# Storing zeros in 22 steps, and holding the first weights of a layer's experts back: a change to a four-layer attention and mixture-of-experts kernel

## The chip, the cores and the metric

The kernel runs on one core of one Trainium2 chip. The core has five engines that run side by side, each with its own instruction stream in a fixed order: TensorE (PE, matmuls, with its weight loads shown as PEld), VectorE (DVE), ScalarE (ACT), GpSimd (POOL) and SyncE (SP). SP, ACT and POOL also issue DMA transfers; all of these run on the core's 16 DMA engines. An engine that has to wait on a semaphore holds everything behind it in its own stream.

The metric is the device time of one execution in microseconds (us), smaller is better.

## The reference: what is computed

The input `x` (2 sequences of 512 tokens, 256 features) passes four layers. Each adds a cross-attention with a context of 2 x 1024 tokens and then a mixture of 8 experts to the stream:

```python
x = x + L0_xattn(layernorm(x), ctx); x = x + L0_ffn(layernorm(x))   # 16 heads of 64, rotary keys; 1 of 8 experts
x = x + L1_xattn(ctx, layernorm(x)); x = x + L1_ffn(layernorm(x))   # 8 heads of 64; 1 of 8 experts and a shared one
x = x + L2_xattn(layernorm(x), ctx); x = x + L2_ffn(layernorm(x))   # 16 heads of 16, causal; 2 of 8 experts
x = x + L3_xattn(layernorm(x), ctx); x = x + L3_ffn(layernorm(x))   # 16 heads of 16, rotary; 2 of 8 experts
# an expert of layer 2, with gates from the two best logits of a token:
out = out + combine[..., e, None] * (relu(x @ w1[e].T) @ w2[e].T)
```

Everything is computed in float32.

## The kernel before

The 1024 tokens lie as 8 tiles of 128 rows in `X`. Each layer runs in two stages.

**Attention of layer 0.** 16 groups, each two heads of one sequence, run as one stream (`run_stream`, called at the end of the layer's block). A group has 4 steps; step `t` belongs to group `n = t // 4` and has place `u = t % 4` in it. In a step (`unit`) PE makes the scores of two key tiles (L862), ACT takes their exponential into `p` (L867), DVE clips `p` (L868) and adds it up (L873), and PE multiplies the `p` of the step before by the values (L793). Small pieces of other work are put between: the keys of the next group (`keys`: two projections, ACT copies them to `kT`, and SP exchanges the halves of each head into `turned` by four DMAs, L155), which `rotate` (L147 to L149) then combines on DVE and POOL at `u == 2`; and the end of the group before. For that end the sums of the exponentials go through `Inverse`: SP gathers them into a small tile (`inv<-sums`, L166), DVE takes the reciprocal (L169), SP writes it to DRAM (`inv<-inv`, L171) and reads it back spread over the partitions (`rec<-inv`, L174), and POOL multiplies (`divide`, L841). PE's own order is fixed as written (`pe_in_order`).

**Experts.** `slots_of` gives each token a row in a table of slots, 128 rows to a slot, and each slot belongs to one expert. `moe` scatters the normed tokens into the DRAM table `xd` by indirect DMAs from POOL, and then works slot by slot (`slot_tile`): the expert's weights come into a tile `w` (L438, from SP, for the first eight slots; an indirect DMA from POOL for the others), the rows come into `xs` (L447), two matmul stages follow, and the result goes to the table `yd` (layers 0 and 1: a plain store from ACT, L479). Afterwards `combine` gathers each token's row from `yd` (`yg`, L530, POOL) and adds it to `X`. Rows of the tables that no token fills must hold zeros (in layers 2 and 3 with a 257th column that says so). `fill_slots` writes these zeros: it is called in step 5 of layer 0's stream, makes a tile `zeros` of 128 x 257 on POOL, which waits for the queries of group 1 (`G[1]["ready"]`), and issues six DMAs from POOL (L655), of 1920, 128, 1920, 384, 2955.5 and 2955.5 KB.

**From layer 1's experts to layer 2's attention.** After the last slot of layer 1, `ahead16` projects layer 2's keys and values from the context: 8 key jobs (PE, then ACT into one of two tiles `sk`, L553, then a store from ACT to the DRAM tensor `kd`, L554) and 4 value jobs (DVE into `sv`, L601, store to `vd`, L603). Beside it `combine` gathers layer 1's results and DVE and ACT (`rsq`, L62) work out the next layernorm. Then `attend16` starts: it fetches `kT` (L1167) and `v` (L1171) of a group from `kd` and `vd`, transposes the normed rows (`pt`, L1252), projects queries (`pq`), and runs 8 groups. A group has a first pass that finds the maximum of each row (L1281 on PE, L1286 and L1287 on DVE), after which `with_maxima` adds the maxima to the queries (`qA`, L1302, DVE), and a second pass, one group later, with scores (L1338), exponentials (L1339), the causal mask on POOL (L1343) and the product with the values (L1314). At the end of a group the same `Inverse` runs with four small DMAs each way; its reciprocal on DVE and the division on POOL (L1353) are pinned in their engines' order.

**What sets the order of the work.** The kernel is written with a planner that keeps each engine's instructions in one fixed order, drawn up before the run from the program's order and estimated durations: an instruction whose inputs and buffers are free may be put ahead of others that stand earlier in the program. So the loads of layer 2's first four weight tiles (`slot_tile`, `s < 4`; the pool `L2g` has four buffers of them), which stand behind the whole attention of layer 2 in the program, are issued from SP ahead of it. `tc.add_manual_dep` adds an edge by hand: with `Sync` the later instruction waits on a semaphore for the earlier one, with `NoSync` only the order on the engine is fixed.

Of the kernel before, what the change touches and what calls it, by code (L numbers as in the profile page):

```python
# [33 lines left out]
def tile_kernel(ctx: ExitStack, tc: tile.TileContext, d: dict, out: bass.AP):  # L34
# [143 lines left out]
    def add_bias(bias):  # L178
        nc.vector.tensor_add(X, X, bias[:, None, :].to_broadcast([P, TT, D]))
# [223 lines left out]

    def moe(L, ps, hp, ep, rows, slots, wrow, used, F, act, glu, finish, filler=None):

# [29 lines left out]
        def slot_tile(s):  # L435
            w = ep.tile([P, WC], F32, tag="w", name="w")
            if s < E:
                nc.sync.dma_start(w, wd[s * P : (s + 1) * P, :])  # L438
            else:
                nc.gpsimd.indirect_dma_start(  # L440
                    out=w, out_offset=None, in_=wd,
                    in_offset=bass.IndirectOffsetOnAxis(ap=wrow[:, s - E : s - E + 1], axis=0),
                )
# [194 lines left out]

    def fill_slots(ins):

        zeros = const.tile([P, D + 1], F32, tag="zeros", name="zeros")
        z = nc.gpsimd.memset(zeros, 0.0).ins
        tc.add_manual_dep(
            z, ins.name, mybir.DependencyInfo(mybir.DependencyClass.Sync, mybir.DependencyReason.DATA),
            reason="transfers that nothing waits for yet",
        )
        nc.gpsimd.tensor_scalar(zeros[:, D:], c_part, 2.0 * NT, None, ALU.add)
        for L, NS, RW in (("L0", 15, D), ("L1", 15, D), ("L2", 23, D + 1), ("L3", 23, D + 1)):
            rows = NS * P + (2 * NT if RW > D else 0)
            xds[L] = [  # L650
                dram.tile([NS * P, RW], F32, tag=f"{L}xd", name="xd"), dram.tile([rows, D], F32, tag=f"{L}yd", name="yd")
            ]

            for to in xds[L][:1] if RW > D else (xds[L][0], xds[L][1][(E + ALWAYS[L]) * P :, :]):
                nc.gpsimd.dma_start(  # L655
                    to.rearrange("(s p) f -> p s f", p=P),
                    zeros[:, None, 0 : to.shape[1]].to_broadcast([P, to.shape[0] // P, to.shape[1]]),
                )

# [11 lines left out]
    with (  # L671
# [186 lines left out]
        def scores(n, kt):  # L858
# [7 lines left out]
            p = G[n][f"p{kt}"] = tmp.tile([P, 2, N], F32, tag="p", name="p", bufs=5)  # L866
            nc.scalar.activation(p, s1, AF.Exp, scale=0.125)  # L867
            nc.vector.tensor_scalar(p, p, EXP_HI, EXP_LO, ALU.min, ALU.max)  # L868
# [6 lines left out]
        def unit(t, pieces):  # L875
# [25 lines left out]
            if t == 5:  # L901
                fill_slots(G[1]["ready"])
                add_bias(bo)
            for _ in range(3):
                pieces()

        for _ in prep(0, first_keys()):
            pass
        nx, nctx = norm_of(X, 4, 4, True), norm_of(C, 8, 8)
        with pe_in_order():  # L910
# [274 lines left out]
    def attend16(L, params, nkt, causal, rotary, bias, first=None, late=None):  # L1185
# [11 lines left out]
        with (  # L1197
# [17 lines left out]
            G = [dict() for _ in groups]  # L1215
            oTs = {}

# [78 lines left out]
            def with_maxima(n):  # L1296

                pt = bank("nmT")
                for qt in range(4):
                    nc.tensor.transpose(pt[:, qt * P : (qt + 1) * P], nms[n % 2][:, qt, :], ident)  # L1300
                qA = kp.tile([P, N], F32, tag="qA", name="qA")
                nc.vector.tensor_add(qA, pt, G[n]["qT"])  # L1302
                G[n]["qA"] = qA
# [90 lines left out]
            with pe_in_order():  # L1394
                while t <= NG * slots + LAG + 6 or pieces.queue:
# [33 lines left out]
                    elif h % 2 or 2 * pieces.left > slots - h or n >= NG:  # L1429
                        pieces()  # L1430
                    t += 1

    ctxr = ExitStack()
# [36 lines left out]

    attend16("L2", params, 4, True, False, True)
    pre.close()
# [3 lines left out]
    with (  # L1476
# [17 lines left out]

        yd = moe("L2", ps, hp, ep, xn, slots, wrow, used, 1024, AF.Relu, False, plain, next_keys)
        add_results(results(ap, yd, 0, 4), gates, X, range(4))
# [244 lines left out]
```

## Time and profile before

| | |
|---|---|
| median of 3 runs | 2299.71 us (2297.59 to 2301.05) |
| the profiled execution's own time | 2299.66 us |
| its span in the profile | 2297.9 us |
| granted TensorE clock, mean | 0.957 of full |
| PE busy | 2098.3 us, 91% of the span |
| DMA moved | 301.22 MB, mean 131 GB/s |
| of it on SP's queue (q1) / POOL's (q0) / ACT's (q10) | 159.79 / 115.00 / 24.39 MB |

How to read what follows. In a line of the order of time, the columns are the start, the time from the first start to the last end, the engine, the line of the kernel, the operation, what it writes and reads, the number of instructions, and in brackets the idle time ahead of it with what ended it. `SPq` and `ACTq` mark instructions that issue a DMA. In a line of the stage table, the columns are the stretch, its length, the busy time of PE, PEld, DVE, ACT and POOL with their instructions in brackets, the clock that TensorE was granted (1.00 is full), the share of the 16 DMA engines that was busy, and GB/s. A shape such as 128x512 is partitions by elements.

### The profile page before, as it was taken

The page shows a single profiled execution, that of the slowest core. Times are in us where ns is not written, and L with a number is a line of the kernel's source. Part 1 is how long each engine was busy: PE and PEld are TensorE (multiplying, and loading weights), DVE is VectorE, ACT ScalarE, POOL GpSimd, SP SyncE. Part 2 cuts the span into 40 slices and gives each one's busy share as a digit, 9 for nine tenths or more (in the row PEclk, how much of TensorE's full clock was granted, in tenths as well). Part 3 has the DMA queues.
Part 4 walks back from the last instruction along what each step waited for, and adds up shares of the span by engine and source line. Part 5 has one row for each costly group of instructions (what it writes and reads, how often), then busy time and mean ns, then how long its engine had stood idle before and what let it go on. Part 6 is the DMA issues. An engine that isn't in the chain of part 4 may idle for free. (4 is left out here: it accounts for less than half of the span.)

```text
span 2297.9 us, 30714 instructions
## 1 busy us (share of the span) xinstructions
PE 2098.3 (91%) x11892; PEld 1270.5 (55%) x11892; DVE 1088.6 (47%) x2161; ACT 864.4 (38%) x1657; POOL 447.3 (19%) x426
## 2 busy tenths in 40 slices
PE   7899999989998999999897898999699999669996
PEld 3344444448984444554585434589533333569985
DVE  7466766651114665665312675211377773422223
ACT  4344444431114655555111233322125556223333
POOL 3133322210002111211101022312122220021210
PEclk9999999999999999999899899999889999789998
DMA  6511111267845101001455311688410101547872
GB/s 189 157 33 47 33 28 28 87 238 272 308 166 149 47 28 37 28 10 33 171 200 222 129 48 41 215 296 321 140 48 23 35 20 25 238 166 311 315 298 63
DMA packets 104392, 301.22 MB, mean 131 GB/s; under 512 B 23088, under 2 KB 66352, under 8 KB 95536
## 3 DMA queue, kind: packets, MB, share of 16 engines
q1 hardware_dynamic: 76624, 159.79, 20.7%
q0 software_dynamic: 12544, 115.00, 13.5%
q10 hardware_dynamic: 15072, 24.39, 2.8%
q8 instruction: 98, 1.61, 0.3%
q14 instruction: 54, 0.44, 0.1%
HBM read 243.42 MB, written 47.66 MB: 127 GB/s over the span
## 5 line engine op out<-in xcount | busy, mean ns | idle before, releaser
L1339 ACT ACTIVATE p<-s 128x512 f32<-128x512 f32 (+3 forms) x384 | 185.9, 545 | 179.3 <-PE s L1338 118.8
L132 PE MATMUL pa<-sT,w 128*128 128x128 f32 x1920 | 235.9, 277 | 10.2 <-DVE sT L457 4.1
L132 PEld LDWEIGHTS pa<-sT,w 128*128 128x128 f32 x1920 | 227.3, 193 | 18.6 <-ACT sq L1519 5.8
L475 PE MATMUL y<-w,hT 128*128 128x256 f32 x960 | 219.8, 381 | 7.7 <-DVE hT L472 4.9
L1281 PE MATMUL s<-kT,qT 32*128 32x512 f32 (+3 forms) x768 | 217.5, 604 | 9.3 <-DVE nm L1287 4.8
L1338 PE MATMUL s<-qA,kT 32*128 32x512 f32 (+3 forms) x768 | 196.2, 585 | 0.7 <-DVE qA L1302 0.4
L475 PEld LDWEIGHTS y<-w,hT 128*128 128x128 f32 x960 | 177.3, 190 | 32.1 <-DVE hT L472 6.8
L1291 DVE TENSOR_REDUCE mx<-s 128x1 f32<-128x512 f32 x256 | 163.3, 684 | 56.2 <-PE s L1281 35.6
L472 DVE TENSOR_TENSOR hT<-act,pg 128x512 f32<-128x512 f32 x82 | 56.2, 687 | 236.4 <-PE pg L132 208.2
L867 ACT ACTIVATE p<-s 128x1024 f32<-128x1024 f32 x128 | 124.1, 1021 | 101.8 <-PE s L862 101.7
L132 PE MATMUL pg<-sT,w 128*128 128x128 f32 x1312 | 160.2, 275 | 1.7 <-ACT sv L570 1.7
L1026 ACT ACTIVATE p<-s,nm 128x512 f32<-128x512 f32 x192 | 129.3, 685 | 83.5 <-DVE nm L1023 83.5
L132 PEld LDWEIGHTS pg<-sT,w 128*128 128x128 f32 x1312 | 153.4, 192 | 1.9 <-ACT sv L570 1.9
L1023 DVE TENSOR_REDUCE nm<-s 128x2 f32<-128x1024 f32 x96 | 113.2, 1220 | 82.0 <-PE s L1019 81.9
L868 DVE TENSOR_SCALAR p<-p 128x1024 f32<-128x1024 f32 x128 | 109.6, 864 | 86.8 <-ACT p L867 86.8
L149 POOL TENSOR_TENSOR kT<-kT,turned 128x512 f32<-128x512 f32 x62 | 99.8, 1615 | 213.9 <-DVE turned L147 207.1
L793 PE MATMUL o<-p,v 128*64 128x512 f32 x512 | 127.5, 614 | 14.6 <-DVE p L868 14.5
L873 DVE TENSOR_TENSOR acc<-acc,p 128x1024 f32<-128x1024 f32 x96 | 131.8, 1373 | 2.8
L862 PE MATMUL s<-qT,kT 64*128 64x512 f32 x512 | 128.1, 619 | 0.0
L1314 PE MATMUL o<-p,v 128*32 128x256 f32 (+3 forms) x1280 | 106.6, 404 | 6.8 <-POOL p L1343 6.6
L1040 PEld LDWEIGHTS pt<-ident,p 128*128 128x128 f32 x768 | 85.6, 141 | 49.0 <-issue 23.8
L1281 PEld LDWEIGHTS s<-kT,qT 32*128 32x128 f32 x768 | 75.8, 188 | 66.0 <-issue 27.3
(284 smaller groups left out, 2981.5 us busy)
## 6 DMA issues: line engine op xcount, KB each, us to landing
w<-in_L_experts_dram SPq DMA_DIRECT2D x8, 3200.0 KB
w<-in_L_experts_dram SPq DMA_DIRECT2D x8, 3072.0 KB
w<-in_L_experts_dram SPq DMA_DIRECT2D x8, 2048.0 KB
w<-in_L_experts_dram SPq DMA_DIRECT2D x8, 1536.0 KB
kd<-sk ACTq DMA_DIRECT2D x40, 256.0 KB
kT<-kd SPq DMA_DIRECT2D x16, 512.0 KB
turned<-kT SPq DMA_DIRECT2D x60, 128.0 KB
v<-vd SPq DMA_DIRECT2D x12, 512.0 KB
```

The costliest lines, as they stand in the source:

```text
L132: nc.tensor.matmul(ps_ap, lhsT[:, dc, lcols], rhs[:, dc, rcols], start=(dc == 0), stop=(dc == 1))
L475: nc.tensor.matmul(y, hT[:, f, :], w2[:, f, :], start=(f == 0), stop=(f == FT - 1))
L793: nc.tensor.matmul(G[n]["o"][64 * j : 64 * j + 64, :], V[g, b][:, kt, pr * P + 64 * j : pr * P + 64 * j + 64], p[:, j, :], start=(kt == 0) ...
L862: nc.tensor.matmul(s1[:, j, :], G[n]["kT"][r, kt * P : (kt + 1) * P], G[n]["qT"][r, :], start=True, stop=True)
L867: nc.scalar.activation(p, s1, AF.Exp, scale=0.125)
L873: nc.vector.tensor_add(G[n]["acc"], G[n]["acc"], p)
L1023: nc.vector.tensor_reduce(nm[:, qt, :, c], s1, AX.X, ALU.max, negate=True)
L1026: nc.scalar.activation(p[:, j, :], s1[:, j, :], AF.Exp, bias=nm[:, qt, j, c : c + 1], accum_out=l[:, qt, j, c : c + 1],)
L1281: nc.tensor.matmul(s1[:, :w], qT[r, qt * P : (qt + 1) * P], kT[r, c * 512 : c * 512 + w], start=True, stop=True)
L1291: nc.vector.tensor_reduce(mx[:, qt, j, c : c + 1], s1, AX.X, ALU.max)
L1338: nc.tensor.matmul(s2[:, qs], kT[r, kt * P : (kt + 1) * P], qA[r, qs], start=True, stop=True)
L1339: nc.scalar.activation(p[:, j, qs], s2[:, qs], AF.Exp, scale=0.25)
```

## The change

Two parts.

1. `fill_slots` becomes a generator. It is started before the stream: it makes `zeros` on POOL, without the wait for group 1's queries, creates the tables, and lists the regions to fill in pieces of at most 512 rows (22 pieces). Then, in every odd step after step 5, it is handed the last exponential of the step and stores one piece, by a DMA from ACT that stands behind this exponential in ACT's order. The pieces come to 10.5 MB as before.
2. `attend16` returns the first instruction that writes a `qA`. For layer 2, `moe` gets it as `hold`, and the loads of the first four weight tiles wait for it with a semaphore.

```diff
--- before.py
+++ after.py
@@ -401,7 +401,7 @@
 
     ALWAYS = {"L0": 6, "L1": 4, "L2": 11, "L3": 13}
 
-    def moe(L, ps, hp, ep, rows, slots, wrow, used, F, act, glu, finish, filler=None):
+    def moe(L, ps, hp, ep, rows, slots, wrow, used, F, act, glu, finish, filler=None, hold=None):
 
 
 
@@ -435,7 +435,12 @@
         def slot_tile(s):
             w = ep.tile([P, WC], F32, tag="w", name="w")
             if s < E:
-                nc.sync.dma_start(w, wd[s * P : (s + 1) * P, :])
+                x = nc.sync.dma_start(w, wd[s * P : (s + 1) * P, :]).ins
+                if hold is not None and s < 4:
+                    tc.add_manual_dep(
+                        x, hold.name, mybir.DependencyInfo(mybir.DependencyClass.Sync, mybir.DependencyReason.DATA),
+                        reason="not among the transfers that the attention waits for",
+                    )
             else:
                 nc.gpsimd.indirect_dma_start(
                     out=w, out_offset=None, in_=wd,
@@ -636,15 +641,13 @@
     dram = ctx.enter_context(tc.tile_pool(name="slots", bufs=1, space=bass.MemoryType.DRAM))
     xds = {}
 
-    def fill_slots(ins):
+    def fill_slots():
+
 
         zeros = const.tile([P, D + 1], F32, tag="zeros", name="zeros")
-        z = nc.gpsimd.memset(zeros, 0.0).ins
-        tc.add_manual_dep(
-            z, ins.name, mybir.DependencyInfo(mybir.DependencyClass.Sync, mybir.DependencyReason.DATA),
-            reason="transfers that nothing waits for yet",
-        )
+        nc.gpsimd.memset(zeros, 0.0)
         nc.gpsimd.tensor_scalar(zeros[:, D:], c_part, 2.0 * NT, None, ALU.add)
+        todo = []
         for L, NS, RW in (("L0", 15, D), ("L1", 15, D), ("L2", 23, D + 1), ("L3", 23, D + 1)):
             rows = NS * P + (2 * NT if RW > D else 0)
             xds[L] = [
@@ -652,10 +655,18 @@
             ]
 
             for to in xds[L][:1] if RW > D else (xds[L][0], xds[L][1][(E + ALWAYS[L]) * P :, :]):
-                nc.gpsimd.dma_start(
-                    to.rearrange("(s p) f -> p s f", p=P),
-                    zeros[:, None, 0 : to.shape[1]].to_broadcast([P, to.shape[0] // P, to.shape[1]]),
-                )
+                todo += [to[r : min(r + 4 * P, to.shape[0]), :] for r in range(0, to.shape[0], 4 * P)]
+        ins = yield
+        for to in todo:
+            x = nc.scalar.dma_start(
+                to.rearrange("(s p) f -> p s f", p=P),
+                zeros[:, None, 0 : to.shape[1]].to_broadcast([P, to.shape[0] // P, to.shape[1]]),
+            ).ins
+            tc.add_manual_dep(
+                x, ins.name, mybir.DependencyInfo(mybir.DependencyClass.NoSync, mybir.DependencyReason.DATA),
+                reason="transfers that nothing waits for yet",
+            )
+            ins = yield
 
     def psum(tags, name):
 
@@ -864,7 +875,7 @@
                 )
 
             p = G[n][f"p{kt}"] = tmp.tile([P, 2, N], F32, tag="p", name="p", bufs=5)
-            nc.scalar.activation(p, s1, AF.Exp, scale=0.125)
+            G[n]["exp"] = nc.scalar.activation(p, s1, AF.Exp, scale=0.125).ins
             nc.vector.tensor_scalar(p, p, EXP_HI, EXP_LO, ALU.min, ALU.max)
             if kt == 1:
                 G[n]["acc"] = tmp.tile([P, 2, N], F32, tag="acc", name="acc")
@@ -899,13 +910,19 @@
             if t == 0:
                 pieces.add(second_batch(nx, nctx), 9)
             if t == 5:
-                fill_slots(G[1]["ready"])
                 add_bias(bo)
+            if t > 5 and t % 2 and n < len(groups):
+                try:
+                    fills.send(G[n]["exp"])
+                except StopIteration:
+                    pass
             for _ in range(3):
                 pieces()
 
         for _ in prep(0, first_keys()):
             pass
+        fills = fill_slots()
+        next(fills)
         nx, nctx = norm_of(X, 4, 4, True), norm_of(C, 8, 8)
         with pe_in_order():
             run_stream(len(groups), 4, 3, unit, prep, lambda n: 3 + 2 * (groups[n][2] == 0))
@@ -1213,7 +1230,7 @@
 
             groups = [(b, g) for b in range(B) for g in range(4)]
             G = [dict() for _ in groups]
-            oTs = {}
+            oTs, ready = {}, []
 
             def fetch(n):
                 g = groups[n][1]
@@ -1299,7 +1316,7 @@
                 for qt in range(4):
                     nc.tensor.transpose(pt[:, qt * P : (qt + 1) * P], nms[n % 2][:, qt, :], ident)
                 qA = kp.tile([P, N], F32, tag="qA", name="qA")
-                nc.vector.tensor_add(qA, pt, G[n]["qT"])
+                ready.append(nc.vector.tensor_add(qA, pt, G[n]["qT"]).ins)
                 G[n]["qA"] = qA
 
             def product(n, kt, half=None):
@@ -1429,6 +1446,7 @@
                     elif h % 2 or 2 * pieces.left > slots - h or n >= NG:
                         pieces()
                     t += 1
+            return ready[0]
 
     ctxr = ExitStack()
     crp = ctxr.enter_context(tc.tile_pool(name="ctxr", bufs=1, reuse_waits="tile"))
@@ -1468,7 +1486,7 @@
         combine(hp, yd, slots, None, X)
 
 
-    attend16("L2", params, 4, True, False, True)
+    hold = attend16("L2", params, 4, True, False, True)
     pre.close()
     pre, params = params16("L3", True, False)
     ap = pre.enter_context(tc.tile_pool(name="L3a", bufs=1, reuse_waits="tile"))
@@ -1492,7 +1510,7 @@
             ahead16(ps, fp, "L3", params, 8)
             first.update(first_of16(ap, "L3", params, 8))
 
-        yd = moe("L2", ps, hp, ep, xn, slots, wrow, used, 1024, AF.Relu, False, plain, next_keys)
+        yd = moe("L2", ps, hp, ep, xn, slots, wrow, used, 1024, AF.Relu, False, plain, next_keys, hold)
         add_results(results(ap, yd, 0, 4), gates, X, range(4))
         late = results(ap, yd, 4, 4), gates
 
```

## The prediction

> **What bounds the kernel now.** I read the page first, for where TensorE (PE) is not busy; then the stage table of the first 150 us and of 1190 to 1330 us, because the change touches these two places; then, in both, the order of time of PE, SP, ACT and POOL; last the waits in the undisturbed part of layer 0, for the slack that the moved stores will meet.
>
> ```profile
> span 2297.9 us, 30714 instructions
> PE 2098.3 (91%) x11892; PEld 1270.5 (55%) x11892; DVE 1088.6 (47%) x2161; ACT 864.4 (38%) x1657; POOL 447.3 (19%) x426
> 80.00:90.00 10.00, 4.64 (x20) 2.04 (x19) 0.31 (x1) 3.11 (x4) 1.53 (x2) 0.89 0.62 156
> 90.00:100.00 10.00, 5.69 (x16) 1.53 (x16) 9.97 (x8) 1.73 (x2) 7.49 (x4) 0.60 0.00 0
> ...
> 350.00:400.00 50.00, 49.88 (x196) 21.47 (x192) 33.62 (x36) 21.57 (x28) 16.29 (x10) 1.00 0.13 32
> ...
> 1240.00:1250.00 10.00, 5.82 (x14) 2.28 (x12) 0.00 (x0) 0.00 (x0) 2.86 (x3) 0.92 1.01 426
> 1250.00:1260.00 10.00, 5.60 (x8) 1.86 (x8) 5.82 (x22) 2.86 (x4) 5.76 (x7) 0.74 0.59 217
> ```
>
> PE is the bound almost everywhere (49.88 of 50 us in the middle of layer 0's stream). So only a place where PE stands is worth anything: one at 84 us, one from 1245 to 1283 us, both beside a saturated DMA share (1.01 to 1.04). The first, by the order of time of SP and PE:
>
> ```profile
> 62.15 2.01 SPq L166 DMA_DIRECT2D inv<-sums  x2
> 74.43 0.35 SPq L171 DMA_DIRECT2D inv<-inv  x1
> 83.48 1.10 SPq L174 DMA_DIRECT2D rec<-inv  x2
> 84.67 2.46 SPq L155 DMA_DIRECT2D turned<-kT  x4
> ...
> 94.31 1.98 PE L793 MATMUL o<-p,v 128*64 128x512 f32 x4 [9.67 <-DVE p L868]
> ```
>
> The four big zero stores and two small ones, issued by POOL from 39.8 to 55.9 us, hold the DMA engines until 83 us. Meanwhile the inverse's round trip on SP takes 21 us (62.15 to 83.48), where later groups need 4 (212.35, 214.93, 216.38). SP issues in order, so the exchange `turned<-kT`, whose keys were copied by 69.7 us, leaves at 84.67. DVE stands 11.0 us before the rotation, the clipping of `p` is queued behind it, and PE waits 9.67 us for `p`. The second place, by SP, ACT and POOL:
>
> ```profile
> 1233.95 28.37 SPq L438 DMA_DIRECT2D w<-in_L_experts_dram  x4
> ...
> 1246.50 0.95 POOL L530 DMA_INDIRECT yg<-yd,si  x1 [35.32 <-DMA w<-in_L_experts_dram]
> ...
> 1251.09 0.69 ACT L553 ACTIVATE sk<-pk,bk 128x512 f32<-128x512 f32 x1 [11.41 <-DMA kd<-sk]
> 1259.73 0.21 ACT L62 ACTIVATE rsq<-rsq 128x4 f32<-128x4 f32 x1 [2.43 <-DVE rsq L61]
> 1260.51 0.69 ACT L553 ACTIVATE sk<-pk,bk 128x512 f32<-128x512 f32 x1 [0.57 <-ACT rsq L62]
> 1271.23 0.69 ACT L553 ACTIVATE sk<-pk,bk 128x512 f32<-128x512 f32 x1 [7.20 <-DMA kd<-sk]
> ...
> 1278.03 2.07 PE L1252 MATMUL pt<-ident,xn 128*128 128x128 f32 x8 [2.48 <-DVE xn L98]
> ```
>
> The four weight tiles of layer 2 (2048 KB each) leave at 1234, though nothing uses them before the xs of layer 2's experts arrive at about 1480 us. Under them the last `yd` store, issued at 1234.27, lets the gathers start only at 1246.50; in layer 0 the same step took 2.6 us (last `yd` store 681.9, first `yg` 684.5). The `kd` stores hold both `sk` buffers, ACT waits 11.41 and 7.20 us, PE's four PSUM banks fill and PE stops.
>
> **The change part by part.** The sum is made against the profiled execution, 2299.66 us (span 2297.9 and 1.8 around it); the median of the runs shown, 2299.71, is the same.
>
> *Zeros: the burst goes.* PE gets back the gaps 9.67, 0.56 (100.65) and 0.18 (101.91). It also gets back the half clock behind them: eight score matmuls in 2.87 instead of 1.99 us, four product matmuls in 1.98 instead of 1.08, together 1.78. That is 12.2 us. Without the burst the exchange leaves at about 70 us and the rotation has 15 us more than now. The gaps at 52.7 and 54.7 (1.22, 0.90) stay: there DVE is busy 9.90 of 10 us.
>
> *Zeros: 22 smaller stores come.* 10.5 MB in pieces of 512 rows (4+1, 4+1, 6, 6 of them), on every odd step from 7 to 49, one per 13 us, on ACT's queue behind the second exponential of the step. Nothing is queued on a semaphore there: `zeros` is ready long before. ACT's issue: no such store is in the trace; the nearest rows are 0.33 us (`kd`, 256 KB) and 0.52 (`C`, 512 KB from SP in 1 KB rows); 22 x 0.5 = 11 us of ACT. It is covered by ACT's own waits right after that exponential (2.69 us before `kT`, 1.27 before `ou`, at 219.02 and 236.23); without that cover it is at most 11. On the DMA engines a piece takes 512 KB / 284 GB/s (the rate at 60 to 70 us) = 1.9 us, 2.25 at the slowest slice of the burst (233). Who can be hit: in each group's second step the piece starts at about 216.4 (exponential 214.39 + 1.94), the `rec` loads run from 216.38 and the exchange leaves at 219.66. The reader of `rec`, POOL at 219.84, is needed by the matmuls `po` at 224.41, 3.3 us after it ends; behind the exchange POOL's product ends at 227.6 and its sum starts at 230.03, 2.4 us of slack (0.7 in the group at 245, whose sum then has 3.7 before its first scores). So 1.9 us fits. Bounds: 0 (more transfers cannot help) and 22 x 2.25 = 50. I take 1, near the covered end. POOL loses six DMA issues (6.9 us), on no path: its next product at 41.91 waited for its exchange, issued 37.35 to 39.85, anyway. The early memset stands on POOL before anything else is due there; its second step waits for `route`, issued at 16.2, and POOL's next work is at 41.9.
>
> A rule weighed here: the Trainium skill, "DMA: Bandwidth & Descriptors", section "Queues, rings and completion order", says that each DMA engine takes turns packet by packet between the queues that have work. By it a store on POOL's queue would hardly hold up two 2 KB reads on SP's queue, the stall at 84 us would have another cause and stay, and the sum would be about 11 us smaller. The trace differs: those reads, on another queue, kept DVE 11.4 us.
>
> *Hold: the stage before layer 2's attention.* Without the weights the gathers start 2.6 us after 1234.27, at 1236.9, 9.6 us earlier. In ACT's order the square root `rsq` stands between the fourth and the fifth `sk`, and it waits for these gathers: fifth `sk` at 1260.51 - 9.6 = 1250.9. With free stores one `sk` follows another every 1.72 us (layer 3's keys, 1452.32 to 1457.47), so the eighth is at 1256.1 instead of 1271.23. From there to the transposes `pt` it is 6.8 us now, of which 1.8 is half clock (eight value matmuls in 3.57 instead of 1.78). So `pt` comes at 1261.1 instead of 1278.03: 16.9 us. The first `pq` runs in 3.12 us now and 1.91 warm: 1.2 more. Together 18.1. Bounds: 14 if the stores still lose some 4 us, 21 if the planner puts `rsq` behind the keys (then eight keys from 1235.25 take 13.8 us, the values 7.1, and `pt` is at 1257 to 1258).
>
> *Hold: the weights inside the attention.* They now wait for the first `qA`, which ends at 1297.2 by the old clock. What stands behind them on SP: `kT` of group 3 (1313.00) and the inverse's trips (`inv<-ou` at 1317.51, then DVE's reciprocal and POOL's division, both pinned in their engines' order, with the maxima and the masks of PE's work behind them). The earlier fetches leave at 1279 to 1283, before `qA`. 8.39 MB at the 425 GB/s of 1238 to 1250 us are 19.7 us, with 2 for latency they end 21.7 after `qA`; `inv<-ou` comes 20.3 after. It is late by 1.4, and POOL already waits 1.62 us for `rec` at 1328.12, so there is no slack: I take 2. Bounds: 0, and 11 if the rate is the burst's 284 GB/s (31.5 after `qA`). Weights in by 1320 are not missed at 1480.
>
> Sum: -12.2 + 1 - 18.1 + 2 = -27.3; 2299.66 - 27.3 = 2272.4, forecast 2272.
>
> **The rivals.**
> 1. *The weights in front of the attention's own transfers.* Price 11 instead of 2: 2281; if the second weight pair also drags, with `kT` of group 3 late, 2284. For it: one queue, no slack in `rec`. Against: at 1240 to 1250 the same transfers ran at 426 GB/s.
> The Trainium skill, same page and section, says that an engine consumes one ring's descriptors in order; by that rule `inv<-ou` could not pass the weights at all. No row here shows two SP transfers passing or not passing.
> 2. *Each fill costs the stream its own length* (ends slower). Place: the exchange and `rec` of each group, and ACT's exponentials; price up to 2.25 us x 22 = 50: 2299.66 - 27.3 - 1 + 49.5 = 2321. It decides from 28.3 / 22 = 1.3 us each; 0.5 each would give 2282. For it: the burst showed that stores on one queue delay small transfers on another far beyond their size. Against: 2.4 to 3.7 us of slack, and a piece that is over when the exchange leaves.
> 3. *The stall at 84 us stays*: it is only DVE's backlog (9.90 of 10 us busy at 50 to 60). Then 2272 + 11 = 2283. Against: DVE is busy 2.71 of 10 at 60 to 70 and waits.
> 4. *The hold changes nothing*: the planner fills the gap with other transfers, or the stores are slow by themselves. Then 18 - 2 = 16 are missing: 2288. Against: `kd` stores at 1452 to 1471, at 231 to 261 GB/s of total traffic, flow every 1.72 us.
>
> **How the numbers follow.** The forecast's case 0.60 (its own range 2265 to 2279, from the bounds 14 and 21 of the hold and 0 and 3 of the fills and collisions); rival 1 0.12; rival 2 0.13, of which 0.07 with 0.5 us each and 0.06 slower; rival 3 0.06; rival 4 0.05; both gains gone or eaten 0.04. The range 2262 to 2286 takes in the forecast, rivals 1, 3 and the mild 2, and leaves out about 0.15. 0.2% (4.6 us) is about what a measurement of this kernel tells from no change: faster 0.88, same 0.04, slower 0.08 (strong rival 2, and a part of the last case).
>
> **What would show it.** Right: no PE gap over 2 us from 60 to 110; `inv<-sums` to `rec` in about 4 us; POOL's queue smaller by 10.5 MB, ACT's larger; `yg` within 3 us of the last `yd`; no wait of `sk` over 3 us; the four weights issued together some 20 us before `inv<-ou`. Wrong: waits of POOL on `turned` or `rec` that grow on odd steps; `inv`'s reciprocal or POOL's division standing more than 5 us in layer 2's first groups; `sk` still waiting for `kd`.

## The result, and the profile after

The changed kernel takes 2271.27 us (2269.58 to 2272.57) against 2298.65 us before: a ratio of 0.9884, with a 95% interval of 0.9864 to 0.9905. The forecast was 2272, in a range of 2262 to 2286. The profiled execution took 2271.06 us, its span is 2269.0, and the mean granted clock is 0.962 (before: 0.957).

From the page, the span, the busy time of the engines, and the queues of POOL (q0) and ACT (q10):

```profile
span 2269.0 us, 30730 instructions
PE 2087.4 (92%) x11892; PEld 1267.6 (56%) x11892; DVE 1085.2 (48%) x2161; ACT 866.2 (38%) x1657; POOL 438.6 (19%) x420
...
q0 software_dynamic: 9888, 104.49, 12.0%
q10 hardware_dynamic: 25664, 34.90, 4.3%
```

The 10.5 MB of zeros are on ACT's queue now (24.39 to 34.90 MB), and off POOL's (115.00 to 104.49). PE does the same 11892 matmuls in 10.9 us less busy time, at a mean granted clock of 0.962 instead of 0.957. From the stage table (columns as before), the two places that the change touches, and the stretch that holds the 22 stores:

```profile
80.00:90.00 10.00, 10.00 (x44) 3.56 (x43) 9.90 (x10) 5.45 (x7) 3.21 (x2) 1.00 0.24 79
90.00:100.00 10.00, 10.00 (x34) 3.66 (x34) 4.60 (x6) 3.94 (x7) 1.27 (x1) 1.00 0.43 126
...
1270.00:1280.00 10.00, 8.79 (x68) 3.60 (x65) 8.55 (x23) 4.17 (x12) 2.80 (x7) 1.00 1.01 429
...
85.00:385.00 300.00, 299.10 (x1152) 126.02 (x1150) 201.13 (x214) 131.39 (x165) 89.26 (x55) 1.00 0.25 70
```

From 80 to 100 us PE is busy all the time at full clock; before, it was busy 4.64 and 5.69 of 10 us there, at 0.89 and 0.60. Over the 300 us with the stores it misses 0.9 us. The saturated DMA share (1.01), which stood at 1240 to 1250 before, now stands at 1270 to 1280, inside layer 2's attention, and PE works under it.

In layer 0, the order of time of SP, the first inverse and the exchange behind it:

```profile
61.53 1.17 SPq L166 DMA_DIRECT2D inv<-sums  x2
...
66.32 1.10 SPq L174 DMA_DIRECT2D rec<-inv  x2
69.13 2.45 SPq L155 DMA_DIRECT2D turned<-kT  x4
```

From `inv<-sums` to `rec` it is 4.8 us instead of 21.3, and the exchange leaves at 69.13 instead of 84.67. From layer 1's last slot to layer 2's attention, by ACT, POOL and PE (the lines of `sk`, `yg` and `pt`; the first line is the last store of a `yd`):

```profile
1217.29 0.33 ACTq L484 DMA_DIRECT2D yd<-yo  x1
...
1219.77 0.95 POOL L535 DMA_INDIRECT yg<-yd,si  x1 [25.58 <-DMA yd<-yo]
...
1226.78 0.69 ACT L558 ACTIVATE sk<-pk,bk 128x512 f32<-128x512 f32 x1 [2.39 <-DMA kd<-sk]
...
1233.55 0.69 ACT L558 ACTIVATE sk<-pk,bk 128x512 f32<-128x512 f32 x1 [0.28 <-ACT rsq L62]
...
1238.05 0.69 ACT L558 ACTIVATE sk<-pk,bk 128x512 f32<-128x512 f32 x1 [0.94 <-PE pk L132]
...
1244.84 1.63 PE L1269 MATMUL pt<-ident,xn 128*128 128x128 f32 x8 [1.69 <-DVE xn L98]
```

The gathers start 2.48 us after the last store instead of 12.23, the longest wait of `sk` for `kd` is 2.39 instead of 11.41, and PE stands 1.69 us before `pt`.

How the weights held the key stores in the kernel before shows in the packets of the two queues, here from 1240 to 1250 us (queue, packets, MB, share of the 16 engines; q1 is SP's queue with the weights, q10 is ACT's with the key stores):

```profile
q1 hardware_dynamic: 267, 3.85, 90.2%
q10 hardware_dynamic: 270, 0.39, 10.4%
```

Both queues move the same number of packets, as if they took turns, but a packet of the weights is ten times as large. So the stores get a tenth of the engines' time, and the gathers and `sk` wait for them.

In the attention, by SP and POOL:

```profile
1265.36 2.30 SPq L438 DMA_DIRECT2D w<-in_L_experts_dram  x4
...
1285.55 2.46 SPq L166 DMA_DIRECT2D inv<-ou  x4
1290.87 0.34 SPq L171 DMA_DIRECT2D inv<-inv  x1
1292.45 1.72 SPq L174 DMA_DIRECT2D rec<-inv  x4
...
1295.90 1.27 POOL L1370 TENSOR_TENSOR oT<-ou,rec 128x512 f32<-128x512 f32 x1 [1.35 <-DMA rec<-inv]
```

The four weight tiles leave 20.2 us before `inv<-ou`. From `inv<-ou` to the division it is 10.35 us, before 10.61 (1317.51 to 1328.12), and the division's wait for `rec` went from 1.62 to 1.35: nothing is late.

Where the time went, by PE's order: when a mark is reached in each kernel, and what the difference gained since the mark above. A mark is the start of the matmuls named, an attention's end is the start of the routing's first matmul behind it, and the last mark is an end.

| mark on PE | before | after | difference | since the last mark |
|---|---|---|---|---|
| layer 0, first sums of exponentials | 60.47 | 59.84 | -0.6 | -0.6 |
| layer 0, second sums | 101.91 | 88.49 | -13.4 | -12.8 |
| layer 0, end of its attention | 501.10 | 487.10 | -14.0 | -0.6 |
| layer 1, last `y` of the experts | 1231.84 | 1214.85 | -17.0 | -3.0 |
| layer 2, first `pt` | 1278.03 | 1244.84 | -33.2 | -16.2 |
| layer 2, first transposed maxima | 1293.21 | 1261.29 | -31.9 | +1.3 |
| layer 2, end of its attention | 1448.31 | 1413.88 | -34.4 | -2.5 |
| layer 2, last `y` of the experts | 1635.09 | 1603.69 | -31.4 | +3.0 |
| layer 3, first transposed maxima | 1693.85 | 1665.78 | -28.1 | +3.3 |
| last matmul | 2293.65 | 2264.99 | -28.7 | -0.6 |

PE's and DVE's instructions stand in the same order in both kernels. ACT's differ only by the 22 stores, SP's only by the four weight loads, which moved behind the attention's first six fetches.

### The profile page after: what moved, and what is told of

Its sections match the earlier page's. It is cut to its first block, busy times and chain, and to the rows that moved or that the text cites. A ratio compares the mean times of both kernels' runs of the same rounds, so it can differ in the third digit from the quotient of the medians.

```text
span 2269.0 us, 30730 instructions
## 1 busy us (share of the span) xinstructions
PE 2087.4 (92%) x11892; PEld 1267.6 (56%) x11892; DVE 1085.2 (48%) x2161; ACT 866.2 (38%) x1657; POOL 438.6 (19%) x420
## 3 DMA queue, kind: packets, MB, share of 16 engines
q0 software_dynamic: 9888, 104.49, 12.0%
q10 hardware_dynamic: 25664, 34.90, 4.3%
```

## The experiments

Each diff is against the changed kernel, and each ratio is to the kernel before as run beside it. The 95% intervals are about 0.2% either way, so of two variants a difference below some 6 us is not settled by one comparison. Where a trace is read against the changed kernel's, both are profiled executions.

### Each part alone

```diff
 # zeros alone: no hold
-        yd = moe("L2", ps, hp, ep, xn, slots, wrow, used, 1024, AF.Relu, False, plain, next_keys, hold)
+        yd = moe("L2", ps, hp, ep, xn, slots, wrow, used, 1024, AF.Relu, False, plain, next_keys)
```

> Only the zeros' part of the change: the loads of layer 2's weights wait for nothing, as before. Theory (two separate contentions that add up): PE's order has no gap over 2 us between 60 and 110 us; layer 0 ends 14 us earlier as in the changed kernel, and the stage before layer 2's attention is as long as before (from the last expert product of layer 1 to the transposes of layer 2's normed rows 46 us, with ACT waiting over 10 us for a store of keys). Time 12 to 17 us below the kernel before: about 2284. Rival (the two parts share one gain, since SP or the planner's order is what was freed): less than 8 us, or over 20.

Measured: 2282.94 us, 0.994 (0.9921 to 0.9958), 15.3 below before. The second sums of layer 0 come at 89.36, as in the changed kernel (88.49). From layer 1's last `y` to layer 2's `pt` it is 46.31 us, as before (46.19).

The other part alone, with the old `fill_slots` and its six stores from POOL:

```diff
 # the hold alone: the zeros as before
             if t == 5:
+                fill_slots(G[1]["ready"])
                 add_bias(bo)
-            if t > 5 and t % 2 and n < len(groups):
...
-        fills = fill_slots()
-        next(fills)
```

> Only the hold: the zeros go in one burst from POOL as before. Theory: the gap of nearly 10 us before PE's products at 84 to 94 us is there again, with DVE standing 11 us before the rotation; the stage before layer 2's attention takes 30 us instead of 46. Time 13 to 19 us below the kernel before: about 2283. Rival (the stall at 84 us is DVE's own backlog and the zeros' part gained elsewhere): the gap is there in this kernel and in zeros_only alike.

Measured: 2282.83 us, 0.9932 (0.9908 to 0.9956), 15.4 below before. The stage before `pt` takes 30.10 us, as in the changed kernel (29.99). Layer 0 keeps its stall; by SP's and PE's order of time in this kernel:

```profile
62.62 2.03 SPq L166 DMA_DIRECT2D inv<-sums  x2
...
82.17 1.10 SPq L174 DMA_DIRECT2D rec<-inv  x2
83.37 2.46 SPq L155 DMA_DIRECT2D turned<-kT  x4
...
92.66 1.97 PE L798 MATMUL o<-p,v 128*64 128x512 f32 x4 [7.56 <-DVE p L873]
```

The inverse's trip takes 19.6 us and the exchange leaves at 83.37, so the burst of zeros, and nothing that the hold does, makes this stall. The two gains lie in different stages and add up: 15.3 and 15.4, together 30.7, against 27.4 for both in the first comparison and 29.3 in the repetition below. The difference lies within the intervals.

### How large a step's store may be

The stores twice, and four times, as large: each step stores its piece and one (or three) more of the same size to spare tables that nobody reads. The diff is the fourfold one; the doubled one has 1 in place of both 3.

```diff
-        for to in todo:
+        spares = {i: dram.tile(list(to.shape), F32, tag=f"spare{i}", name="spare") for i, to in enumerate(todo * 3)}
+        todo = [[to] + [spares[i + k * len(todo)][:, :] for k in range(3)] for i, to in enumerate(todo)]
+        for to, step in ((to, step) for step in todo for to in step):
...
-            ins = yield
+            if to is step[-1]:
+                ins = yield
```

> The changed kernel, in which every step stores its piece of zeros twice, the second time to a spare table that nobody reads: 21 MB instead of 10.5 through the same 22 steps, 3.8 us of transfer in a step instead of 1.9, and twice the issues on ACT. Theory (a piece is hidden as long as it is over before the next exchange, some 3 us after it starts in the second step of a group): as the changed kernel, to 5 us above it, with PE still over 99% busy in the middle of layer 0. Rival (each piece costs the stream a part of its own length, 0.5 to 2.25 us): 11 to 50 us above the changed kernel.

Measured, doubled: 2271.8 us, 0.9891 (0.9864 to 0.9917). The second 512 KB of a step cost nothing that the times can tell. In the traces, the stretch from the second to the fifteenth sums of layer 0 takes 351.7 us without any store (the kernel with the hold alone, whose burst is over by then), 351.8 with one piece a step and 353.2 with two.

> The changed kernel in which every odd step stores its piece of zeros four times, three of them to spare tables: 2 MB and some 7.4 us of transfer in a step, one after another from ACT, where the doubled kernel had 3.8 us and cost nothing. Theory (a store costs as far as it lasts into an exchange or an inverse's trip, which leave 3 us after the start of the piece or 7 us): 10 to 40 us above the changed kernel. Rival (the slack of a step is larger than 7 us): within 3 us of it.

Measured, fourfold: 2290.45 us, 0.9969 (0.9953 to 0.9986), some 19 above the changed kernel's 2271.27 and 21.7 above its repetition. In the profiled execution (2298.92 us) the same stretch takes 375.5 us, 23.7 more than in the changed kernel. The durations of the single issues, lowest, median and highest in ns, in the changed kernel, the doubled and the fourfold one (there those of the spare tables), each from the list of a tile's instructions:

```profile
L661 ACTq DMA_DIRECT2D xd<-zeros x20: 366/366/387, 83.1 to 364.8; - x20
```
```profile
L663 ACTq DMA_DIRECT2D spare<-zeros x22: 444/520/520, 83.8 to 366.9; - x22
```
```profile
L663 ACTq DMA_DIRECT2D spare<-zeros x66: 387/1049/1513, 84.8 to 387.0; - x66
```

And the fourfold kernel's first step with a store, by SP's and PE's order of time:

```profile
91.51 1.15 SPq L166 DMA_DIRECT2D inv<-sums  x2
...
98.75 1.12 SPq L174 DMA_DIRECT2D rec<-inv  x2
...
107.29 4.92 PE L864 MATMUL po<-wo,oT 128*128 128x256 f32 x14 [2.74 <-POOL oT L855]
```

From `inv<-sums` to `rec` it is 7.2 us instead of 4.1 (90.22 to 94.29 in the changed kernel), and to POOL's product 13.9 instead of 8.0, so the matmuls behind it come late; that is rival 2's mechanism, at four times the size. Of PE's waits between 85 and 445 us, 14.4 in all, 11.0 stand in front of `po`, for POOL's product. The mean DMA share from 85 to 385 us is only 0.57, so it is not the mean load that tells whether a trip is hit. In the same steps ACT itself stands 2.4 to 4.0 us while it issues the three further stores; how much of the loss comes by this way was not separated.

The other way to make them larger: the six whole regions as six stores, one in each odd step.

```diff
-                todo += [to[r : min(r + 4 * P, to.shape[0]), :] for r in range(0, to.shape[0], 4 * P)]
+                todo.append(to)
```

> The changed kernel with whole regions instead of pieces: six stores of 1920, 128, 1920, 384, 2955.5 and 2955.5 KB from ACT in the odd steps 7 to 17, the same bytes, at 284 GB/s 7 us for the second largest and 11 us for the largest. Theory (what hurts is a store that lasts into a round trip of the stream): the last of them starts 3 us before an exchange and holds it up by up to 8 us, the one before it meets the sums of the next group; 2 to 10 us above the changed kernel, the lost time as PE gaps in 130 to 170 us. Rival (only a queue of all 10.5 MB at once hurts): no gap, the same time as the changed kernel.

Measured: 2283.1 us, 0.9929 (0.9903 to 0.9954), 11.8 above the changed kernel: more than the theory gave. In the trace the loss is one event. The mark of the third sums is 0.7 us behind the changed kernel's, that of the sixth 11.05, that of the eleventh 11.04. By ACT's, SP's and PE's order of time there:

```profile
138.00 0.37 ACTq L661 DMA_DIRECT2D xd<-zeros  x1
...
145.16 1.87 SPq L166 DMA_DIRECT2D inv<-sums  x2
...
148.35 0.37 ACTq L661 DMA_DIRECT2D xd<-zeros  x1
...
158.10 1.10 SPq L174 DMA_DIRECT2D rec<-inv  x2
...
164.11 4.99 PE L861 MATMUL po<-wo,oT 128*128 128x256 f32 x14 [5.91 <-POOL oT L852]
```

The two stores of 2955.5 KB, one behind the other, keep the engines full from 138 to 159 us (mean DMA share 1.00), and the inverse in this time takes 12.9 us instead of 4. It is the old stall again, from ACT's queue instead of POOL's.

### When the weights may leave

Earlier: the hold is the last addition of layer 1's results (`combine`), so the weights stay behind the gathers but are under way with the keys' stores.

```diff
-                    nc.vector.tensor_add(to, to, yg)
+                    x = nc.vector.tensor_add(to, to, yg).ins
...
-        combine(hp, yd, slots, None, X)
+        hold = combine(hp, yd, slots, None, X)
```

> The changed kernel, but the four weight tiles of layer 2 wait only for the last sum of layer 1's results into X, not for the first qA: they leave after the gathers and before the last four stores of keys and the four of values, and on SP ahead of the first fetch of keys and values. Theory (the weights cost what stands beside and behind them: stores on ACT's queue that share the engines, fetches on SP's queue behind 20 us of weights): the gathers stay as early as in the changed kernel, the first scores of layer 2's attention come 5 to 12 us later than there, time 5 to 12 us above the changed kernel. Rival (only the late gathers cost time before): within 2 us of the changed kernel.

Measured: 2289.43 us, 0.9954 (0.9937 to 0.9972), 18 above the changed kernel, well over what was expected. Layer 2's `pt` comes 18.8 us later than in the changed kernel. From layer 1's last `y` to it the stage takes 47.0 us, where the kernel before has 46.2: the whole gain of the hold is gone. By POOL's, SP's and ACT's order of time:

```profile
1221.56 0.95 POOL L535 DMA_INDIRECT yg<-yd,si  x1 [25.59 <-DMA yd<-yo]
...
1233.75 14.08 SPq L438 DMA_DIRECT2D w<-in_L_experts_dram  x4
...
1245.39 0.69 ACT L559 ACTIVATE sk<-pk,bk 128x512 f32<-128x512 f32 x1 [9.09 <-DMA kd<-sk]
...
1256.01 0.69 ACT L559 ACTIVATE sk<-pk,bk 128x512 f32<-128x512 f32 x1 [7.46 <-DMA kd<-sk]
```

The gathers start 2.5 us after the last `yd` store (1219.08), as early as in the changed kernel, and it helps nothing: the stores of the keys, under the weights, make ACT wait 9.09 and 7.46 us.

Later: the hold is the second group's `qA`.

```diff
-            return ready[0]
+            return ready[1]
```

> The changed kernel, but the weights wait for the second group's qA instead of the first's: one leaves about 5 us before the inverse's trip of the first group, the others stand on SP between the steps of the trips of the first two groups. Theory (a trip that finds 2 MB ahead of it on its own queue loses the 5 us that these take): the spread inverse of the first two groups comes 5 to 15 us later after its sums than the 10 us of the changed kernel, POOL's division waits for it and PE with it, 4 to 15 us above the changed kernel. Rival (what is queued on SP ahead of a small transfer does not hold it up): within 2 us of the changed kernel.

Measured: 2275.05 us, 0.991 (0.9879 to 0.9941), about 4 above the changed kernel, which the intervals alone do not tell from nothing. In the trace, layer 2's maxima go from 3.6 us ahead of the changed kernel's (the first) to 5.4 behind (the last), so 9.0 are lost within this attention. By SP's order of time:

```profile
1287.48 0.33 SPq L171 DMA_DIRECT2D inv<-inv  x1
1287.91 0.38 SPq L438 DMA_DIRECT2D w<-in_L_experts_dram  x1
1292.78 1.72 SPq L174 DMA_DIRECT2D rec<-inv  x4
...
1297.16 2.83 SPq L166 DMA_DIRECT2D inv<-ou  x4
1305.87 0.33 SPq L171 DMA_DIRECT2D inv<-inv  x1
```

One weight tile leaves ahead of this trip's second step (at 1284.42) and one right behind it: from `inv<-inv` to `rec` it is 5.30 us instead of 1.58. The second group's gather takes 8.71 instead of 5.3. This is the collision of rival 1, at the place where the weights do meet the trips.

### Is it one queue, or the engines?

Here the collision is made on purpose from another queue. When the second group's `qA` is ready, ACT copies four weight tiles of 2 MB from DRAM to spare DRAM tables that nobody reads; the hold stays on the first `qA`.

```diff
                 ready.append(nc.vector.tensor_add(qA, pt, G[n]["qT"]).ins)
+                if L == "L2" and n == 1:
+                    for i in range(4):
+                        spare = dram.tile([P, 4096], F32, tag=f"spare{i}", name="spare")
+                        x = nc.scalar.dma_start(spare, d["L2_experts"][i * P : (i + 1) * P, :]).ins
+                        tc.add_manual_dep(x, ready[1].name, ...)
```

> The changed kernel with four more transfers: copies of 2 MB each of layer 2's experts into a spare table that nobody reads, issued from ACT when the second group's qA is there, so that 8.4 MB run on ACT's queue beside the inverse's trip of the first group and of the second on SP's queue. Theory (what the burst of zeros showed: a saturated set of engines holds small transfers on any other queue for 9 to 11 us a step): the first group's trip lasts 10 us or more longer than in the changed kernel and PE loses 5 to 15 us there. Rival (engines take turns between queues, packet by packet, so a small transfer on another queue passes): trip longer by at most 2 us a step, time within 3 us of the changed kernel.

Measured: 2298.98 us, 0.9994 (0.9977 to 1.001), 28 above the changed kernel. By SP's, DVE's and ACT's order of time:

```profile
1278.53 2.54 ACTq L1323 DMA_DIRECT2D spare<-in_L_experts_dram  x4
...
1283.03 13.17 SPq L166 DMA_DIRECT2D inv<-ou  x4
...
1311.55 0.25 DVE L169 RECIPROCAL inv<-inv 128x16 f32<-128x16 f32 x1 [22.86 <-DMA inv<-ou]
1311.83 0.34 SPq L171 DMA_DIRECT2D inv<-inv  x1
```

Four gathers of 2 KB on SP's queue need 28.8 us from the first issue to `inv<-inv` (5.3 in the changed kernel), with 8 MB more on ACT's queue. So a different queue does not keep a bulk transfer out of a trip's way. But the run does not clear the trip's own queue either. The held weights are still moving on it when the copies start. SP's two longest waits from 1278 to 1312 us for a transfer (line, what it waited for, us in total, times, longest), and the packets of the two queues from 1290 to 1306:

```profile
SPq L171 <- DMA inv<-ou: 15.1, 1, 15.1
SPq L166 <- DMA w<-in_L_experts_dram: 10.8, 1, 10.8
```
```profile
q10 hardware_dynamic: 113, 5.18, 95.4%
q1 hardware_dynamic: 113, 0.24, 5.0%
```

The profile puts the 10.8 us between the second and the third gather down to the landing of a weight tile. Behind that, SP's queue and ACT's move one packet each in turn, 113 and 113, but ACT's have 46 KB on average and SP's 2 KB. So what stands ahead of the trip on its own queue (the last weights and a fetch of keys) goes at the pace of the copies, and the trip behind it. What the copies would do to a trip with nothing ahead of it, this run does not show.

The copies added 8.4 MB to ACT's queue in 192 packets, 44 KB each on average (25664 packets in the changed kernel, 25856 here); in the trace 128 of them have 64 KB. So the same amount was tried as zeros from SBUF in rows of 1 KB, which make 8256 packets: four stores of 2048 rows, at the same place, again to spare tables (`small_rows[0]` is the tile `zeros`). The rows of the copies are 16 KB; the 64 KB in the expectation are those packets.

```diff
+                        spare = dram.tile([16 * P, D], F32, tag=f"spare{i}", name="spare")
+                        x = nc.scalar.dma_start(
+                            spare.rearrange("(s p) f -> p s f", p=P),
+                            small_rows[0][:, None, 0:D].to_broadcast([P, 16, D]),
+                        ).ins
```

> As the run with four copies of 2 MB on ACT's queue beside the inverse's trip, but the four transfers write zeros from the tile of 128 x 257 into a spare table in rows of 1 KB, where the copies had rows of 64 KB: the same 8.4 MB, the same queue, the same place. Theory (what holds a small transfer on SP's queue is the saturated set of engines, whatever the rows): the first group's trip from the gathering to its reciprocal lasts over 15 us instead of 5.3, PE loses 8 to 20 us. Rival (engines take turns between the queues, and only large rows make a turn long): 5 to 9 us, PE loses under 4 us.

Measured: 2296.85 us, 0.9995 (0.9981 to 1.001), 26 above the changed kernel; the loss is as large, but it came by another way. By ACT's, PE's and SP's order of time:

```profile
1279.92 20.94 ACTq L1324 DMA_DIRECT2D spare<-zeros  x4
...
1301.72 0.65 PE L1343 MATMUL o<-p,v 128*32 128x128 f32 x8 [19.15 <-POOL p L1372]
...
1303.05 5.00 SPq L166 DMA_DIRECT2D inv<-ou  x4
1312.35 0.34 SPq L171 DMA_DIRECT2D inv<-inv  x1
```

ACT is held 20.94 us by the four issues themselves, so the exponentials behind them come late, and `inv<-ou` is issued only when the weights and 6.1 of the 8.4 MB of zeros have moved. The trip then takes 9.3 us to `inv<-inv`, and 2.1 MB of zeros still pass on ACT's queue from 1303 to 1309, at a DMA share of 1.04. So a trip that starts beside small rows lost 4.0 us, 2.5 of them because SP's four issues took 5.00 us instead of 2.46; but the zeros end within this trip, and how long it would take under all 8 MB is not settled. With the burst of the kernel before, zeros from POOL's queue in packets of 4 KB (2656 packets for the 10.5 MB), its two steps took 12.3 us (62.15 to 74.43) and 9.1 (to 83.48).

### A third tile for the values, and the kernel again

In the trace of the changed kernel ACT waits 6.22 us before an `sv` (1465.21), until the store `vd<-sv` of the same tile has landed; it holds the ReLU behind it, and PE stands 5.26 us before a `y`. A third `sv` tile is to take the wait away.

```diff
-        vs = [st.tile([P, 2, 16, 32], F32, tag=f"sv{i}", name="sv", bufs=1) for i in range(2)]
+        vs = [st.tile([P, 2, 16, 32], F32, tag=f"sv{i}", name="sv", bufs=1) for i in range(3)]
...
-            v = vs[n % 2]
+            v = vs[n % 3]
```

> The changed kernel with three tiles instead of two for the values on their way to DRAM, ahead of the attention of layers 2 and 3. In the changed kernel ACT waited 2.28 and 6.22 us for a store of values before the first products of layer 2's experts, with 5.26 us of PE behind it. Theory: these two waits shrink and the kernel gains 1 to 5 us: 2266 to 2270. Rival (the stores' own rate sets the end of the values, the number of tiles only moves the wait): within 1 us of the changed kernel.

> The kernel with three value tiles once more, beside the changed kernel on one chip. If its gain is real, it is 3 to 7 us below the changed kernel, with the stretch from layer 2's routing to the last product of its experts some 5 us shorter than the 190 us there. Rival: the earlier difference was run to run, and they lie within 2 us.

> The changed kernel once more, beside the others on one chip: 2268 to 2275, and a second trace of it to see how much a stage varies from run to run without any change; a stage may differ by some 2 us, the stage before layer 2's attention again takes about 30 us.

Measured: 2266.39 us, 0.9852 (0.9828 to 0.9876), and again 2264.43 us, 0.985 (0.9827 to 0.9872); the changed kernel beside the second one 2268.71 us, 0.988 (0.9858 to 0.9903). Both times it is 4 to 5 us below the changed kernel (the first time below its 2271.27 us, which were measured on another occasion), the lowest median of all kernels here, but the intervals overlap. The two profiled executions took 2271.76 and 2270.88 us, no less than the changed kernel's (2271.06 and 2266.36), so the trace can't place the gain, and it is not shown to be one. What it shows: ACT's waits for `vd` at this line fall from 13.3 to 3.6 and 2.9 us, and from the end of layer 2's attention to the experts' last `y` it is 185.0 and 184.9 us instead of 189.8. Ahead of that, the attention from its first transposed maxima to its end takes 157.8 us instead of 152.6, which takes the gain away again in these two executions. But with two tiles the same stretch took 152.5 to 158.0 us in other kernels here, so that loss is not tied to the third tile.

## Why the prediction was right, point by point

**The zeros' burst (-12.2 forecast): -13.4 at the second sums.** The chain was as described: burst, inverse's trip, exchange, rotation, `p`. The zeros alone remove it, and the hold alone keeps it. Of the 13.4, 0.6 lie ahead of the first sums: the gap at 52.7, which was to stay, went from 1.22 us to 0.71. Rival 3 (the stall is only DVE's backlog) fell: DVE is busy 9.90 of 10 us at 80 to 90, and PE doesn't wait.

**The 22 stores (+1 forecast, bounds 0 and 50): 0.** An issue takes 0.366 us where 0.5 was taken, and PE misses 0.9 of 300 us. (POOL's six issues had taken 7.1 us and not 6.9, on no path.) The slack of 2.4 to 3.7 us was real: a step takes twice the bytes for 1.5 us over all 22 steps. Rival 2 fell at this size, in its mild form too, but its reason (stores on one queue delay small transfers on another) is right, and shows in the larger stores: 2 MB a step cost 19 to 22 us over 22 steps, two stores of 3 MB 11 in one place.

**The stage before layer 2's attention (-18.1 forecast): -16.2 at `pt`, -14.9 with what follows.** Counted from the last `yd` store, the forecast and the trace are: gathers 2.6 and 2.48; fifth `sk` 16.6 and 16.26; eighth `sk` 21.8 and 20.76; `pt` 26.8 and 27.55. Half a clock gone between the last key and `pt` was taken as 1.8 us; the time there stayed at 6.79, since the values' stores now end the wait (1.92 for `vd`). The 1.2 us of the first `pq` came (2.01 instead of 3.12), but were lost at the next projection, which now runs at half clock (four matmuls in 3.37): -33.2 at `pt` became -31.9 at the first maxima. These two terms of the clock were mis-sized by 3 us. One step was incomplete as well: the forecast took the gathers as the start of the chain and the keys' stores as what follows it. The early-hold experiment shows the stores as a limit of their own: with early gathers, and the weights only under the stores, all is lost. Rival 4 fell: the stage is 16 us shorter with the hold alone too.

**The weights inside the attention (+2 forecast, bounds 0 and 11): 0.** The forecast had `inv<-ou` come 20.3 us after `qA` and the weights end after 21.7; it came 20.2 us after the weights' issue, and was not late. The forecast charged 2 us for an overlap that cost nothing: by the trace's packets the weights end at 1288.4, 23.1 us after their issue and 2.9 into the trip, and yet the trip takes 5.32 us to `inv<-inv`, as in the next group (5.31). So rival 1 stayed away by a small margin, and the later hold shows what it costs where the weights do stand between a trip's steps. Its reason, one queue, is only a part of it: 8 MB on ACT's queue, beside the end of the weights on SP's, delayed the trip by 23.5 us. The attention itself came out 2.5 us shorter (first transposed maxima to its end, 155.1 before and 152.6 after). That is no gain of the hold that could be shown: in kernels that hold the weights alike, the stretch takes 152.5 to 158.0 us, and its last part, from the last maxima on, 39.5 at a mean granted clock of 0.91 and 44.9 at 0.77.

**What the forecast did not have.** 3.0 us were gained between layer 0's attention and layer 1's last `y`, where no instruction differs, and 5.7 were lost again behind layer 2's attention. For the first, the granted clock: from layer 0's last `y` to layer 1's first scores it is 46.09 us before, at a mean granted clock of 0.96 and with PE busy for 40.73, and 44.04 after, at 1.00 and busy for 39.03. The changed kernel's repetition has 45.93 there, again at 0.96, so these 2 us come and go without any change; the other 1.0 was not looked into. For the second, 3.0 lie in the experts of layer 2, from the end of the attention to the last `y`: 186.8 before, 189.8 after, 189.7 in the repetition, 190.4 with the hold alone and 188.9 with the zeros alone. One wait of PE changes by as much, that of the `y` behind the store of values that the third tile was for: 1.81 us before, 2.19 with the zeros alone, 4.40 with the hold alone, 5.26 and 5.20 with both. So the loss comes with the hold, but not always: the run with copies holds the weights too, and has 1.65 for this wait and 186.6 for the stretch. The cause stays open. The other 3.3 are not there in the repetition (58.76 before, 62.09 after, 58.89 again). So that 2272 is within 1 us of 2271.27 is partly chance: the terms were off by 1 to 3 us each, in both directions.

**The rule that was weighed.** By the Trainium skill, "DMA: Bandwidth & Descriptors", section "Queues, rings and completion order", a DMA engine goes from queue to queue packet by packet. The traces agree, counted in the profile's packets: where SP's and ACT's queue both have work, they move the same number of packets, 267 and 270 in the kernel before (1240 to 1250), 113 and 113 beside the copies, 37 and 37 when the small zeros meet the weights (1284 to 1286). What failed is what the forecast drew from it, that a small transfer then hardly waits, and its "the trace differs" holds for this alone. Each packet of a small transfer, and of what stands ahead of it on its own queue, gives a turn to a packet of the other queue, and these can be large: 16 KB of weights for 2 KB of keys, 46 KB of a copy for 2 KB of a fetch. That is not the whole of it. Beside stores with rows of 1 KB a trip still took 12.9 us instead of 4, and what holds it there no run settles.

## What to carry to other kernels

Look for a short round trip (a few KB out and back through DRAM) that starts while a bulk transfer is under way, on whatever queue; its price is the trip's new length plus everything queued behind it on its engine. Cut the bulk into pieces that are over before the next trip starts: here 1 MB per step cost next to nothing, and 2 MB cost 19 to 22 us. Release a prefetch that nobody needs soon at the start of a stretch in which no store or trip ends a wait: here a group later lost 9.0 us in the trace of that attention, and a stage earlier 18 us.

## What was not expected of the hardware

Issuing can hold the engine that issues. One store of 512 rows took ACT 0.366 us, the second in a row 0.520, and the further ones in the fourfold kernel 1.049 at the median and 1.513 at most. Four stores of 2048 rows of 1 KB took 20.94 us: the first 0.37, the others 8.86, 6.04 and 5.56. Yet a single store of 2955.5 KB in rows of about 1 KB was issued in 0.37 us. So the time seems to depend on what is still in the queue or on the engines, and not on the size of the store; that was not tested by itself.
